# A transformer block on one core: the rotation of the queries' and keys' weights moves from VectorE and GpSimd to TensorE

## The chip, the core and the metric

The kernel runs on one core of one Trainium2 chip. The core has five engines with a queue of instructions each: TensorE (PE in the profile, with its weight loads as PEld), VectorE (DVE), ScalarE (ACT), GpSimd (POOL) and SyncE (SP), which here issues every DMA. An engine works through its own queue in order; engines wait for each other only through semaphores. Matrix products land in PSUM, everything else lives in SBUF. The metric is the device time of one execution in microseconds (us). Three runs of the kernel before gave 1052.85, 1056.75 and 1058.46 us, median 1056.75 us.

## The reference

Inputs are `x` (8, 512, 512) and the weights of one attention layer and one feed-forward layer, all in fp32. Cut to what matters:

```python
x = x + layernorm(attention(layernorm(x)))
x = x + layernorm(ffn(layernorm(x)))

# attention: 16 heads of 32; q, k, v from x @ w_attn + b_attn (512 x 1536)
q = rope(q); k = rope(k)            # the angle depends on the head and the pair, not on the token
p = softmax(causal(q @ k.T)) * 512**-0.5
out = (p @ v) @ w_proj + b_proj

def rope(a, b):                     # the two values of a pair of columns
    return a * cos - b * sin, a * sin + b * cos

# ffn: both weights made ternary (sign(round(w / mean|w|)) * mean|w|), rows normalised and
# quantised to 128 steps of their largest value, exact gelu in between
```

The rotation's angles are indexed by head, so the rotation is a fixed linear map of the columns of the projection. The kernel therefore turns the columns of `w_attn` for queries and keys once, ahead of all tokens, and never turns a query or a key.

## The kernel before, in words

The whole block runs as one program over 8 sequences of 512 tokens. `prepare_x` normalises 128 rows of `x`, splits them into an fp16 high and low half and has them transposed (by TensorE for the first sequence, L494, by transposing DMAs after it, L501). `queries_keys` makes queries and keys of a group of 4 heads with 12 fp16 products each (L553), `values` the values (L523). `maxima` makes the scores of four heads (L588, in `sc` tiles of PSUM) and takes them to SBUF with the row minima by a VectorE pass (L602). `probabilities` exponentiates (ACT, L639), rounds to fp16 (ACT, L645), takes the remainder (POOL, L647) and has both transposed by DMA. `weighted` multiplies by the values (L674), `gather` and `project` follow (L719). The feed-forward part is `ff_front`, `ff_expand` (L805, gelu L814), `ff_quantise` (L828, L839, L843, L756, L761) and `ff_contract` (L861).

The weights are prepared on the way. `make_v_weights` and `make_proj_weights` scale and split the other attention weights; `magnitude` (ACT, L410) reads the feed-forward weights a first time for their mean, and `ternarize` (POOL L446, ACT L449) makes them ternary on a second reading.

The queries' and keys' weights are made in eight pieces, one for queries (s = 0) and one for keys (s = 1) of each of four head groups g, of 512 x 128 each. `load_qk` loads one as `wraw`. `make_qk_weights(s, g)` takes the squares (ACT, L231), sums them over all 512 rows with a product by ones (PE, L240, and a one-column fp32 product for the bias, L241), turns the weights (`rotate`, L203 to L205: six passes over 128 x 256 values, by VectorE for queries and by GpSimd for keys), derives a power-of-two scale that bounds the longest column (VectorE, L249 to L256 and L170), and splits the scaled weights into two fp16 halves `wqk` (ACT L259, DVE L261). The cosines and sines lie in `cs`, spread over all partitions by one DMA (L888); `bcol` and `rcol` hold the bias and the angles with one column of weights per partition.

What sets the order of the work is the string `ORDER`: one letter is one step of one stream of work (H: queries' weights, J: keys' weights, N: `prepare_x`, T: `magnitude`, Y: `ternarize`, S: `maxima`, A: `probabilities`, X: `ff_expand`, and so on). Steps are traced in that order, and `pin` ties each instruction to the one before it on its engine, so that each queue is exactly the string's order:

```python
for k in "".join(ORDER.split()):
    step(k)
```

PSUM is shared by three `sc` tiles of two banks and two `mm` tiles of one bank. `sc` tiles are used by scores, by the product with the values and by `ff_expand`; `mm` tiles by all other products. The pool tag `x1` has five buffers and holds `wraw`, `rot`, `cs` and later rows of `x`; the tag `ph1` has two buffers for probabilities.

Of the kernel before, what the change touches and what calls it, by code (L numbers as in the profile page):

```python
# [10 lines left out]
F32 = mybir.dt.float32  # L11
# [8 lines left out]
P = 128  # L20
# [16 lines left out]
nnwwwNBtRNHnnwHHHHtttNNJJNNNNBNJJBBHBBBBwJRNHJBHwNNNJBBNTNBNHNNNNRRRHRHRBTttHHNNTwtNBRNNJTtRNHNN  # L37
TtTtJHHJJJNNTtTtHTtBQJRNNQHHHQJTtQQQJQJQTHQHQTJJTBJwQYtIttQQBQQBQJHHHTRQtTtHQSQnSHwnYYQTtYQYQAHS
YYSYtAASQYNVQYHnntrYYAAVtANVVAYYtJSSQQAAQQYQQQQAAAJJAQQVSAVVVVQVQYNtYAJAAJVAJVVVYtVAASAAArVVNSSn
AVWWJSVVVJVAAAAYVASVVVASAAAYVStSQWQQWYWWAAVAAASWAQQQQQQVVQNYYWWNNSWWWAAAAAWNNNNNVRSAAYSNSASNNWYA  # L40
QtNtVQAAAAAWARNAASAAASVVSWWYRNNNSWGSGWWWWWWWWWAAAAAAVVVVYSVVAAVVASAVWQAQAAAGGYYVVVWSWANVVSAAQSGG
QSASAQAAAAAWSWWAAQWQQQQRSWWWWWNWAAAAQWQWAYQYAAQASGAQSRQAQASAAARStQQnQQtSWWQWAAASWWWQSVGGWWWQWWWR
WWQAVAAYAGYGGSAQQAAVAAAQAVQAASQSSSQQAQAQAAQPAPYYAPPPtPQPASSAPPFAFAVPNVVVSSAPPPAFASAAAVWPVVPFFWQW
WWAQFFWVAWnANAnQQVQWWVWQQQQQNWNSYYSVPVFSWPAWAANASYNFPQNNAPAAAAAAAWNNAAAGXFAPFNNASNSAQXXFFSGXXXXX
XNXPWZrnNAnWWWAWWPVNNNWSAVASWWWWWZWVXZZVAAAAVWZPSAAAAXXVZVAFAZAZXZQSQQQSAVQSANXQQXQNPrXXPXPSPGGA
FAXGASQWPSPWZAWFQZQWWWAAAWWWGVQWWWWWVVSAQZVAZrASCAZGQZGQAAAAAZSZQQAAACSSPCZAAAACQSCZACVWVCVPFZZS
VSCAPAAAAAAQWQGWAAQSWQQWACSQACWQWCQWFASAWWWWWWSACQCZAGGVVVGSVAAQFASQQQNNAAWQQWQAQSVnQVAAVVSPVAPV
AAAAVSPVWWWCZWSPSQWWWWQWWAASFFFPQWAAAXAQXASAAXAZZAWFZAQAQQSQVXZZAPVQAPSXXWPQNNNXXAVNSNVPQWFQCXWP
WWPWAPCZFnNNFNXSFAFGFZZCFGWrAWPWCVCWCWWVWNAAZNZNNZNZFSnAACXAAZZVVSNVNWNCCVSAAAFZVPCAFVFXPXFQCSXQ
SAAACVASPAQASAAAAVVQVQXXQNZQXXAAPNSZZXPXSQXPZXCCZrPQZZSWWWPWACQACAZXCAAAAWXCWCFZAFAAPZPZQSXQFPPS  # L50
FZFFSAPZACPGACXGCGWWWWWPZXXSCZPVZGZCAAXWCZCXZACCFCFVFCWZAZZSCVAVQCQWCWQCZAQZSCAASWSACAAAGQQQSXAQ
WWWCWQNAnXQGWWWWWWWAANACCAAAAZACVAGrCPFSZWXQVSFPQFrFFGVVVSXGXGVVVVZXPFZVPXSPZAXAVZSVQFPQAAAAAAAS
PQPFWQAAAAQZQQXPXSQZZZZZCCQCQCSWWWCFFSFWWCFWPWWWWAAAWCAQQZAVWVASASCWAVVQCZSCQnAZAAXQSXXSQZZCACAA
PAAAAACSPACASXAQZPAAAQCXXZGPXXQPWPGQXCWQWQWCWZWZFNNrXXCXXZZZWWCWWWWNCAWCXFCAFPPQAAAAZZQFVFFFPNNN
NCNVnAZXXZWSXZXNZCCnCCPZCCNrNNSVZVFZXZPZZZNCPXCSXPAASNZZAPCVXCXANNASPAVSCZSACPAAZAAVZVVCZZZSVASC
ASAAAAVVQAXCCAAASCAQCSXWWQVCQFXVQFXQPWPZVrWWVQCPQNZWQPZZQAAGGZXPZAGWSANGAAQXQACPQSWWFQWXQWWQCWFC
FFZFZASSAACWWSAAZAAACQZWQFZZPCQXCQCWWWWSPXQGGZGZXQFAAAAnAAWASAAAXCCFNFCFSFSCVWWWWWVZAQAPXXWXXVCA
QWGZnZVVXSQNrXAZAGXQVQFGFSSSAQCZZVZXXAQAVVAQZSAAFQZVQVVAAXQCWQCAWCZZFAQAQFPCXSPCWCWWSPZFCPCAASAZ
PXWZZFZCAAACZZZXAAAXAWAAVXACSCVSQZPPVVSPSPAQPQWCCPWWPWWXArAZZAAQQZSPCFWFQCZAZZZQCQAACQWCZFAAQNPA
ASCWCQNWCPXGWWWXWSPQXVNAAAFCNGCZNAFWWWWWWWnZAAFFVNNWNACVXSZVVSCZNSPVAPNACSVVSFNAACFrASNPACAAAAAA  # L60
AAPPCXXCXFANXCXACZXNSZSZZNCZNPVSCVAXFFAnCVZCCAVAAAPCCAXXSZXSFQFXPFNPZCCQAPZSQWQZWXWWXFrXWXWPGGQG
# [17 lines left out]
ZZWWCWWWWWWWWGGGCXCZZZZXXCCZCXXZPCCPPPZZPPCPFrCCZCCPZZFZFFFXXZXCCPZZZFFCXCXZCFPXrZXCCZZCCZPZXZCr  # L79
PPPZPZPFFFFXZPPPPPFCPZFZZPPFCXCFXCCXZZZXZZPXFCXCXXZZFPZCXFCCFCFZXFZCXPZXCXXPCrZPZXXXPPZPZCZZZFCZ  # L80
XXFZXXZFFZZFZFCCCFCXCCCCCCZXZCZZCXCZZZZZCXCXCXXZZZZZXXCZXCXCXCCZCZZCZZCCCCXCCXCXCZCCXZXZZZCCCZZZ
CZCCCZZZZZZZCCCCCCCCCCCCCCCCCCCCCCCCCCCCC
"""


# [937 lines left out]
```

## Time and profile before

| what | value |
|---|---|
| median of three runs | 1056.75 us (1052.85 to 1058.46) |
| the profiled execution | 1060.78 us, its span 1059.0 us |
| busy: PE, DVE, ACT, POOL | 973.7, 842.0, 907.2, 795.2 us |
| first scores on PE (L588), first pass over them on DVE (L602) | 54.70 us, 55.65 us |
| first exponential on ACT (L639) | 57.31 us |
| first gelu on ACT, with its table load (L814) | 192.82 us |
| DMA packets' time, as a share of 16 engines' span | 90.7% |

Times in the profile count from the start of the span. A digit of the 40 slices is the busy share of some 26 us in tenths. In tables by stretch, each engine has its busy time in that stretch and the number of its instructions; PEclk is the granted TensorE clock as a share of full speed. A busy PE is an upper bound, since ends of matmuls are modelled. One fp32 product shows as two records, each with its own weight load; one fp16 or bf16 product shows as one.

### The profile page before, as it was taken

How to read it: one execution, taken by the hardware profiler on the slowest of the kernel's cores; microseconds unless marked ns; L12 is line 12 of the kernel's file. 1: busy time of each engine (PE TensorE's matmuls, PEld its weight loads, DVE VectorE, ACT ScalarE, POOL GpSimd, SP SyncE). 2: the span in 40 equal slices, each digit the busy share in tenths (PEclk: the TensorE clock that was granted, in tenths of full speed). 3: DMA queues.
4: the chain of work that ended last, by engine and by line, in shares of the span. 5: the costliest groups of instructions: out<-in, count | busy, mean ns of one | idle time of the engine just before them, and what ended most of it. 6: DMA issues, size and time to landing. Idle time of an engine off the chain costs nothing.

```text
span 1059.0 us, 22837 instructions
## 1 busy us (share of the span) xinstructions
PE 973.7 (92%) x8170; PEld 499.2 (47%) x8170; DVE 842.0 (80%) x2652; ACT 907.2 (86%) x1492; POOL 795.2 (75%) x648
## 2 busy tenths in 40 slices
PE   4677789998999999999999999999999999999995
PEld 2344445444545554555545455454454444444441
DVE  7988869898888788787988887797878788866651
ACT  4788989999799997999999999889899889964552
POOL 6888989888786777885888687767867768865543
PEclk9898889999999999999999999999999999999997
DMA  8779999999998998999999999899998979995452
GB/s 288 259 230 201 221 192 206 193 203 186 181 183 151 200 169 167 192 182 175 187 189 176 179 183 169 160 168 195 176 170 161 170 135 182 193 191 126 100 109 70
DMA packets 588498, 189.74 MB, mean 179 GB/s; under 512 B 564576, under 2 KB 568672, under 8 KB 588384
## 3 DMA queue, kind: packets, MB, share of 16 engines
q1 hardware_dynamic: 588384, 188.28, 90.7%
q8 instruction: 64, 1.05, 0.4%
q14 instruction: 50, 0.41, 0.1%
HBM read 38.29 MB, written 8.39 MB: 44 GB/s over the span
## 4 chain that ended last, share of the span: by engine, by line
PE 33%; ACT 15%; POOL 14%; DVE 13%; DMA 11%; issue 8%; SPq 1%; POOLq 0%; ACTq 0%; DVEq 0%
PE sc L805 10%; PE mm L861 7%; POOL ph L647 6%; PE mm L553 5%; ACT p L639 5%; DMA pT<-ph 4%; PE mm L719 4%; DVE p L602 4%; DMA qT<-q 3%; PE mm L523 3%; ACT ph L645 3%; PE sc L674 3%; PE sc L588 2%; POOL h L839 2%; DMA xT<-hT 2%
## 5 line engine op out<-in xcount | busy, mean ns | idle before, releaser
L647 POOL TENSOR_TENSOR ph<-p,ph 128x768 f16<-128x768 f32 (+1 forms) x192 | 353.0, 1841 | 81.8 <-ACT ph L645 69.2
L602 DVE CUSTOM_DVE_ANT_0 p<-sc,mask,e_scale 128x384 f32<-128x384 f32 (+3 forms) x512 | 255.4, 545 | 22.7 <-POOL ph L647 13.7
L861 PE MATMUL mm<-wout,qT 128*128 128x512 fp8e4 x1024 | 259.4, 382 | 7.9 <-DMA qT<-q 6.0
L805 PE MATMUL sc<-wfc,qT 128*128 128x512 fp8e4 x1024 | 254.7, 380 | 2.6 <-DMA qT<-q 2.4
L639 ACT ACTIVATE p<-p,nmax 128x384 f32<-128x384 f32 (+3 forms) x512 | 254.2, 551 | 2.0 <-DVE nmax L613 1.4
L553 PE MATMUL mm<-xT,wqk 128*128 128x512 f16 x768 | 207.2, 389 | 10.2 <-DVE wtop L250 3.4
L645 ACT CAST ph<-p 128x768 f16<-128x768 f32 (+1 forms) x192 | 172.6, 899 | 4.3 <-DMA pT<-ph 0.8
L805 PEld LDWEIGHTS <-qT 128*128 128x128 f16 x1024 | 97.4, 98 | 116.0 <-issue 7.9
L861 PEld LDWEIGHTS <-qT 128*128 128x128 f16 x1024 | 94.9, 98 | 118.6 <-issue 13.8
L674 PEld LDWEIGHTS <-pT 128*128 128x128 f16 x2560 | 99.0, 98 | 57.8 <-DMA pT<-ph 16.8
L674 PE MATMUL sc<-vt,pT 128*128 128x65 f16 (+1 forms) x2560 | 103.7, 187 | 12.1 <-DMA pT<-ph 9.9
L553 PEld LDWEIGHTS <-wqk 128*128 128x128 f16 x768 | 70.6, 100 | 90.4 <-issue 24.0
L523 PE MATMUL mm<-wv,xT 128*128 128x256 f16 x768 | 104.0, 276 | 4.9 <-DVE src L567 1.9
L839 POOL TENSOR_SCALAR h<-h,hnm,hqs 128x1024 f32<-128x1024 f32 x64 | 79.0, 1235 | 37.9 <-DVE hnm L835 37.8
L719 PE MATMUL mm<-wp,oT 128*128 128x512 f16 x384 | 102.0, 379 | 5.7 <-DVE row L730 1.6
L523 PEld LDWEIGHTS <-xT 128*128 128x128 f16 x768 | 73.2, 99 | 34.9 <-issue 11.2
L761 POOL TENSOR_TENSOR q<-h,q 128x1024 f16<-128x1024 f32 x32 | 69.7, 2178 | 26.5 <-ACT q L756 24.0
L588 PE MATMUL sc<-src 32*128 32x128 f16 (+3 forms) x1536 | 76.0, 303 | 13.8 <-DVE low L602 10.7
L828 DVE TENSOR_REDUCE htop<-h 128x1 f32<-128x1024 f32 x64 | 76.5, 1211 | 5.5 <-ACT h L814 5.5
L756 ACT CAST q<-h 128x1024 f16<-128x1024 f32 x64 | 66.5, 1039 | 16.6 <-POOL h L839 15.6
L814 ACT ACTIVATE h<-sc,fsc 128x1024 f32<-128x1024 f32 x64 | 71.0, 1110 | 7.4 <-PE sc L805 7.0
L843 ACT ACTIVATE junk<-h 128x1024 bf16<-128x1024 f32 x64 | 67.3, 1052 | 11.1 <-DMA qT<-q 10.2
(156 smaller groups left out, 1378.7 us busy)
## 6 DMA issues: line engine op xcount, KB each, us to landing
row<-in_x SPq DMA_DIRECT2D x32, 256.0 KB, 3.5
tw<-in_w_fcT SPq DMA_DIRECT2D x16, 512.0 KB, 5.5
tw<-in_w_outT SPq DMA_DIRECT2D x16, 512.0 KB, 4.8
x<-in_x SPq DMA_DIRECT2D x32, 256.0 KB, 3.6
out<-row SPq DMA_DIRECT2D x32, 256.0 KB, 2.8
wraw<-in_w_attn SPq DMA_DIRECT2D x8, 256.0 KB, 5.1
pT<-ph SPq DMA_TRANSPOSE x128, 5.5
qT<-q SPq DMA_TRANSPOSE x96, 4.3
```

What stands on the lines that cost most here:

```text
L523: nc.tensor.matmul(ps[:, :256], xT[:, c, hx, k, :], wv[hw][:, k, half * 256 : (half + 1) * 256], start=(n == 0), stop=(n == 3 * NE - 1),)
L553: nc.tensor.matmul(ps, w[:, hw, k, :], xT[:, :, hx, k, :], start=(n == 0), stop=(n == 3 * NE - 1),)
L588: nc.tensor.matmul(scs[j // 2][:, j % 2, at : at + (i + 1) * P], src[rows, hq, ts(i, P)], src[rows, hk, : (i + 1) * P], start=(m == 0), st ...
L602: nc.vector.tensor_tensor_reduce(p[:, j, at : at + (i + 1) * P], scs[t][:, j, at : at + (i + 1) * P], mask[:, T - (i + 1) * P :], e_scale[ ...
L639: nc.scalar.activation(pj, pj, AF.Exp, bias=nm[:, i, 2 * t + j : 2 * t + j + 1], scale=-1.0)
L645: nc.scalar.copy(hi, p)
L647: nc.gpsimd.tensor_tensor(lo, p, hi, ALU.subtract)
L674: nc.tensor.matmul(oo[:, j, i, :width], probs[u, PARTS[i]][:, half, j, STARTS[i] + c, :], vt[c][:, h, :width], start=(n == 0), stop=(n == ...
L719: nc.tensor.matmul(ps, oTs[b, k][:, ho, i, :], wp[hw][:, k, :], start=(n == 0), stop=(n == 3 * NE - 1),)
L805: nc.tensor.matmul(ps[:, o1, :], xsT[0][:, n // NE, n % NE, :], wfc[:, n % NE, ts(o, 512)], start=(n == 0), stop=(n == 2 * NE - 1),)
L839: nc.gpsimd.tensor_scalar(hh, hh, nm, s, ALU.add, ALU.mult)
L861: nc.tensor.matmul(ps, hT[0][:, half, k, :], wout[:, o2 * NF // 2 + k, :], start=(n == 0), stop=(n == 2 * NF - 1),)
```

## The change

`make_qk_weights` no longer turns the weights by elementwise passes. Four fp32 products by an identity transpose the piece into PSUM (four blocks of 128 x 128, a product with `turns[:, NG]`). ScalarE copies the transposed piece to SBUF (`wT`) and squares it with a running sum along the free axis, which gives the squared length of each column. Four more fp32 products, of `wT` with `turns[:, g]`, transpose back and turn in one: `turns[:, g]` has the cosines on its diagonal and the sines beside it, built once from `rcol` by VectorE in `qk_biases`. VectorE puts the squared lengths, with the bias added, on a diagonal (`diag`, bf16), one product by ones spreads them over all partitions, and the reduction to the largest and the scale follow as before, with one pass less. The two fp16 halves are made from the turned weights in PSUM.

`rotate`, the tile `cs` and its DMA are gone. `turns` takes a buffer of tag `ph1`. Each piece takes two `sc` tiles of PSUM, where it took one `mm` tile. `wT` takes the place of `rot` in tag `x1`. `ORDER` is another string over the same steps, shown here by its first line alone; a weight piece still takes seven steps.

```diff
-nnwwwNBtRNHnnwHHHHtttNNJJNNNNBNJJBBHBBBBwJRNHJBHwNNNJBBNTNBNHNNNNRRRHRHRBTttHHNNTwtNBRNNJTtRNHNN
...
+nnnwwwBRwNHHNwttwtNNHJHJNNJNHJNNBBBBBBBNBNHNJRwRRNBBHHntNHNHNNJHTtRJRJHJRRNTJNNBNNJtHNBNTtNHHHHN
...
@@ -180,29 +180,33 @@
     bcol = const.tile([P, 5 * NE], F32)
     rcol = const.tile([P, 4 * NE], F32)
     bqk = const.tile([P, 2 * NG], F32)
-    cs = x1p.tile([P, 2, E // 2], F32, tag="x1", name="cs")
+
+
+    turns = pp.tile([P, NG + 1, P], F32, tag="ph1", name="turns", bufs=2)
 
     def qk_biases():
 
         n = 2 * NE
-        t = tiny(n, "bt")
+        t = tiny(n + NG, "bt")
+        t, nsin = t[:, 0:n], t[:, n : n + NG]
         nc.vector.tensor_tensor(bqk, bcol[:, 0:n], rcol[:, 0:n], ALU.mult)
         nc.vector.tensor_tensor(t, bcol[:, n : 2 * n], rcol[:, n : 2 * n], ALU.mult)
         nc.vector.tensor_tensor(bqk, bqk, t, ALU.add)
-        yield
-
-    def rotate(dst, w, c, s, eng):
-
-        wv = w.rearrange("p s (f two) -> p s f two", two=2)
-        dv = dst.rearrange("p s (f two) -> p s f two", two=2)
-        a, bb = wv[:, :, :, 0], wv[:, :, :, 1]
-        shape = [P, w.shape[1], w.shape[2] // 2]
-        c, s = (t[:, None, :].to_broadcast(shape) for t in (c, s))
-        for n, (x1, x2, op) in enumerate(((c, s, ALU.subtract), (s, c, ALU.add))):
-            t = pp.tile([P, 2, *shape[1:]], F32, tag="p", name="rope", bufs=3)
-            eng.tensor_tensor(t[:, 0], a, x1, ALU.mult)
-            eng.tensor_tensor(t[:, 1], bb, x2, ALU.mult)
-            eng.tensor_tensor(dv[:, :, :, n], t[:, 0], t[:, 1], op)
+
+
+        nc.vector.tensor_copy(turns[:, NG, :], ident_h)
+        for g in range(NG):
+            nc.vector.tensor_scalar(turns[:, g, :], ident_h, rcol[:, g : g + 1], None, ALU.mult)
+            pairs = turns[:, g, :].rearrange("p (f two) -> p f two", two=2)
+            ones_at = ident_h.rearrange("p (f two) -> p f two", two=2)
+            sine = nsin[:, g : g + 1]
+            if g == 0:
+                nc.vector.tensor_scalar(nsin, rcol[:, n : n + NG], -1.0, None, ALU.mult)
+            for two in range(2):
+                nc.vector.scalar_tensor_tensor(
+                    pairs[:, :, two], ones_at[:, :, 1 - two], sine, pairs[:, :, two], ALU.mult, ALU.add
+                )
+        yield
 
     wr = w_attn.rearrange("(c p) f -> p c f", p=P)
     wqk = {
@@ -227,30 +231,32 @@
 
 
         n = s * NG + g
-        sq = tp.tile([P, NE, P], BF16, tag="q", name="sq", bufs=2)
-        nc.scalar.activation(
-            sq.rearrange("p c f -> p (c f)"), w.rearrange("p c f -> p (c f)"), AF.Square
-        )
-        yield
-        b2 = tiny(name=f"b2{s}")
+        pst = sc_tile()[:, 0, :]
+        for k in range(NE):
+            nc.tensor.matmul(pst[:, ts(k, P)], w[:, k, :], turns[:, NG, :], start=True, stop=True)
+        yield
+        wT = x1p.tile([P, E], F32, tag="x1", name="wT")
+        sq = tp.tile([P, E], BF16, tag="q", name="sq", bufs=2)
+        longest = tiny(2, f"long{s}")
+        nc.scalar.copy(wT, pst)
+        nc.scalar.activation(sq, pst, AF.Square, accum_out=longest[:, 0:1])
+        yield
+        b2 = longest[:, 1:2]
         nc.vector.tensor_tensor(b2, bqk[:, n : n + 1], bqk[:, n : n + 1], ALU.mult)
-        yield
-        ps = mm_tile()
+        nc.vector.tensor_scalar(b2, longest[:, 0:1], 2.0 * E, b2, ALU.mult, ALU.add)
+        diag = tp.tile([P, P], BF16, tag="qT4", name="diag", bufs=2)
+        nc.vector.tensor_scalar(diag, ident_h, b2, None, ALU.mult)
+        yield
+
+        ps = sc_tile()
+        rot = ps[:, 0, :]
         for k in range(NE):
-            nc.tensor.matmul(ps[:, 0:P], ones_b, sq[:, k, :], start=(k == 0), stop=(k == NE - 1))
-        nc.tensor.matmul(ps[:, P : P + 1], ones, b2, start=True, stop=True)
-        yield
-        rot = x1p.tile([P, NE, P], F32, tag="x1", name="rot")
-        at = slice(g * P // 2, (g + 1) * P // 2)
-        rotate(rot, w, cs[:, 0, at], cs[:, 1, at], nc.gpsimd if s else nc.vector)
-        rot = rot.rearrange("p c f -> p (c f)")
+            nc.tensor.matmul(rot[:, ts(k, P)], wT[:, ts(k, P)], turns[:, g, :], start=True, stop=True)
+        nc.tensor.matmul(ps[:, 1, 0:P], ones_b, diag, start=True, stop=True)
         yield
         top, sc = tiny(name=f"wtop{s}"), tiny(name=f"wsc{s}")
-        nc.vector.tensor_reduce(top, ps[:, 0:P], AX.X, ALU.max)
-        nc.vector.scalar_tensor_tensor(
-            top, top, 2.0 * E, ps[:, P : P + 1], ALU.mult, ALU.add
-        )
-        nc.vector.tensor_scalar(top, top, 2.02, 2.0**-60, ALU.mult, ALU.max)
+        nc.vector.tensor_reduce(top, ps[:, 1, 0:P], AX.X, ALU.max)
+        nc.vector.tensor_scalar(top, top, 4.04, 2.0**-60, ALU.mult, ALU.max)
         root_power(top, top)
         nc.vector.reciprocal(sc, top)
         nc.vector.tensor_scalar(sc, sc, 2.0 ** (12 - 65) / X_S, None, ALU.mult)
@@ -885,10 +891,6 @@
 
 
     def load_ropes():
-        nc.sync.dma_start(
-            out=cs.rearrange("p a f -> p (a f)"),
-            in_=rope.rearrange("a f -> (a f)").partition_broadcast(P),
-        )
         nc.sync.dma_start(out=bcol, in_=b_cols)
         nc.sync.dma_start(out=rcol, in_=rope_cols)
         yield
```

## The prediction, made before the changed kernel ran

> **What bounds the kernel now.** I read the page's slices first, then busy time by stretch, then the rows of the first 60 us, where the edited steps lie.
>
> ```profile
> PE   4677789998999999999999999999999999999995
> DVE  7988869898888788787988887797878788866651
> ACT  4788989999799997999999999889899889964552
> POOL 6888989888786777885888687767867768865543
> PEclk9898889999999999999999999999999999999997
> ```
>
> From the seventh slice (about 160 us) PE stands at nine tenths or more, with one exception, to the last but one; ACT comes near, with sevens between. Before that PE is at four to eight tenths, and its granted clock is mostly short of full. So the span is a ramp, in which PE waits for the others, and a long stretch that PE bounds. Cutting the span at the first pass over scores (55.65 us), at the first gelu's table load (192.80 us) and near the end gives (columns: stretch, its length, PE, PEld, DVE, ACT, POOL, clock, DMA share, GB/s):
>
> ```profile
> 0.00:55.65 55.65, 30.59 (x154) 15.62 (x155) 46.46 (x129) 34.89 (x60) 41.08 (x60) 0.91 0.81 270
> 55.65:192.80 137.15, 111.00 (x1128) 62.69 (x1128) 113.89 (x412) 126.06 (x218) 120.35 (x92) 0.90 1.02 208
> 192.80:1000.00 807.20, 786.02 (x6692) 401.05 (x6691) 658.74 (x2054) 724.78 (x1184) 610.15 (x476) 1.00 0.94 175
> ```
>
> I call the first two A and B. In the third PE is busy 786.02 of 807.20 us, 97.4%: what the change saves off PE there is worth nothing, and what it does in A and B moves the start of that stretch and with it the end. In B ACT is busy 92%, POOL 88%, DVE 83%, with the DMA engines' share at 1.02: four resources nearly level, ACT first. A in stretches of 8 us shows one engine ahead:
>
> ```profile
> 8.00:16.00 8.00, 4.19 (x20) 2.02 (x19) 7.55 (x24) 4.96 (x9) 7.23 (x9) 1.00 1.01 366
> 16.00:24.00 8.00, 4.22 (x12) 1.85 (x13) 7.69 (x24) 3.07 (x6) 5.34 (x4) 1.00 1.05 360
> 24.00:32.00 8.00, 5.89 (x26) 2.82 (x23) 7.06 (x18) 5.75 (x11) 7.16 (x6) 1.00 0.53 159
> 32.00:40.00 8.00, 3.82 (x19) 2.07 (x19) 7.79 (x19) 7.17 (x14) 7.03 (x9) 0.62 0.72 222
> 40.00:48.00 8.00, 5.31 (x28) 2.54 (x27) 7.67 (x19) 7.65 (x14) 6.74 (x17) 0.95 0.94 320
> ```
>
> DVE is the third number: 7.06 to 7.79 of 8 us in all five. PE is at half, ACT between, POOL at 5.3 to 7.2. So A is DVE's queue, and the chain of waits agrees: from 39 us to 48.8 us it lies on DVE alone, through rotation, scale and second halves of weights, before it passes to PE.
>
> **The change, part by part.** The rows that price it:
>
> ```profile
> 22.95 0.41 DVE L203 TENSOR_TENSOR rope<-wraw,cs 128x256 f32<-128x256 f32 x1
> 23.29 0.41 DVE L204 TENSOR_TENSOR rope<-wraw,cs 128x256 f32<-128x256 f32 x1
> 23.73 0.88 DVE L205 TENSOR_TENSOR rot<-rope 128x256 f32<-128x256 f32 x1
> 26.50 0.28 DVE L249 TENSOR_REDUCE wtop<-mm 128x1 f32<-128x128 f32 x1
> ...
> 17.32 1.06 ACT L410 ACTIVATE tw<-tw 128x1024 f32<-128x1024 f32 x1
> 18.28 0.19 ACT L410 ACTIVATION_READ_ACCUMULATOR tw<-tw 128x1 f32 x1
> ...
> 18.34 2.02 PE L339 MATMUL mm<-wpraw,bv 128*128 128x512 f32 x2
> 28.70 1.13 PE L339 MATMUL mm<-wpraw,bv 128*128 128x512 f32 x2
> ...
> 49.67 0.98 PE sc L314 x8
> ```
>
> *DVE in A.* Rotation of a query piece runs from 22.95 to 26.50 us, 3.55 us; the others take 3.64 (6.75 to 10.39), 3.43 (38.83 to 42.26) and 3.0 us (six rows at 50.83 to 53.8), together 13.6 us, all ahead of the first pass over scores. Added ahead of that pass by the new order: `turns`, five full passes of 128x128 at 0.28 us (the bias passes L335, 0.28 at their least), eight half passes at 0.22 (between 0.28 and the 0.15 of a one-column pass) and one of 0.15, 3.3 us; seven `diag` passes at 0.28, 2.0 us; seven one-column passes for the squared length against six of L250 that go, 0.15; and, moved forward, one more second half (L261, 0.75), its four small passes (0.6) and one row's statistics (0.69 and three small ones, 1.1), 2.4 us. Sum -13.6 + 3.3 + 2.0 + 0.15 + 2.4 = -5.7 us. The halves now read PSUM: L567 (PSUM in, same shape) has 0.74 beside L261's 0.75, on ACT L565 0.68 beside L259's 0.72, so nothing for that.
>
> *PE in A.* Out go 28 products by ones and 7 of one column; a piece's five take from 0.46 us (at 45.68 us) to 0.82 us (from 24.68 to 25.50), so 3.2 to 5.7 us. In come 28 transposes and 24 turns ahead of the first scores, fp32, 128x128, which no row shows. From below: four fp32 products with one weight row and one column take 0.98 us back to back (49.67 us), 0.25 each. From above: the 512-column product at 18.34 us takes 2.02 us at the slow clock, a quarter 0.51. So 13.0 to 26.5 us and 0.5 for six products by ones; net between +10.3 (13.5 - 3.2) and +21.3 (27 - 5.7). PE is busy 29.9 us ahead of the first scores at 54.70, so 24.8 us are idle, 7.4 of them before any weights have landed. With no other gap PE would come to its first scores at 7.4 + 29.9 + 10.3 = 47.6 us at the least, or 58.6 with 21.3. I take 0.35 a product, nearer the lower row, since the same 512-column product took 1.13 us at 28.70, 0.28 a quarter, and a fuller PE should hold that pace more often: 18.2 + 0.5 - 4.4 (the middle of what goes) = +14.3, 51.6 us.
>
> On the clock the rows are: four fp16 transposes in 0.61 us at 16.20 and 17.94, in 0.39 at 27.23 after 2.5 us of near steady products, in 0.63 again at 37.81 after two idle stretches over 2 us. [...] No fp32 product of this shape is in the trace to decide.
>
> *POOL.* Six passes a key piece, 24 in all at some 0.74 us, 17.8 us go; 18 of them lie in A. The last of the rows that the first queries need are split on POOL at 33.53 us, behind one rotated piece (9.27 to 14.02, 4.8 us) and two passes of L306; the new order has no rotation and one L306 ahead. They can come some 7 us sooner, but I take nothing for it, since DVE and PE then set the end of A.
>
> *ACT.* Per piece a copy from PSUM (0.65, between 0.58 for L496 and 0.72 for L259) and a square with its running sum (0.62 + the 0.19 that an accumulator read takes at 18.28) replace a square of 0.62: +0.84, eight times 6.7 us, all ahead of the first exponential in the new order. A has 20.8 idle us on ACT, 4.2 of them one wait for POOL at 18.5, so this is covered there. But four of the sixteen passes of L410 now stand behind the first exponential: 4 x 1.04 = 4.2 us more in B, less one square and one eviction (0.9) that left it: +3.3.
>
> *Queues and buffers.* SP loses one issue of 0.42 us (`cs`); a load of `x` takes its place, so the first `wraw` is no earlier. The other DMAs are the same; three of the second readings of the feed-forward weights go behind the first transposes, whose place in SP's queue is so much sooner. Pieces six and seven take four `sc` tiles between scores; a turned piece holds its tile until DVE has made its second half, and the next scores wait. That is two holds; the score waits for DVE in the trace (L588 for `low` L602) are 10.7 us over 8, 1.3 each: 0 to 2.6, I take 0 because the products of L523 and L553 stand between. `turns` holds one of two `ph1` buffers until the last turn, which stands ahead of the first cast into that tag: nothing, and if late one cast (1.04).
>
> *The sum.* A ends by DVE at 55.65 - 5.7 = 49.95, by PE's first scores at 51.6 plus 0.95 to the pass = 52.55, -3.1. PE's 29.9 us were in part at the slow pace too and would shrink, so I take a value between, -4. B: POOL's share there loses 3.0 (six rotations out, 4.4, one row's preparation out, 2.9, four L352 in, 4.3), ACT's rises 3.3 with 11.1 us idle to hide it: 0 to 3.3, I take +1. From the gelu on, order and work are the same kinds in the same numbers, so -3 reaches the end: span 1056, execution 1057.8 against 1060.78. The median of the runs stands 4.03 us below the profiled execution; 1056.75 - 3 = 1053.75, say **1053.5 us**.
>
> **The rivals.**
>
> *Faster by more.* Several DVE rows in A are far above their least: L261 once 2.63 against 0.75, L335 twice 1.0 against 0.31, L267 0.92 and 0.50 against 0.15, with POOL active at each. That is 1.9 + 1.4 + 1.1 = 4.4 us. If a lighter POOL ends these, PE's other products speed up as well, and B hides its addition, A ends 5.7 + 4.4 = 10.1 us sooner: 1046.7. Against it: the POOL passes beside four of these five rows are L306, L310 and L510, which stay; and PE would have to start its first scores at 44.6, under its least.
>
> *Slower: PE becomes the bound of A.* The place is PE's queue ahead of the first scores. At price p PE arrives there no sooner than 7.4 + 29.9 - 4.4 + 0.5 + 52p; that passes 54.70 at p = 0.41. At 0.51, with 5.7 taken out, it is 58.6, +3.9; with the middle of B's bounds, 1.7, it makes +5.6: 1062.4. For it: PE's clock in A is short of full in several rows. Against it: rows near 27 and 43 us are fast as soon as PE is busy.
>
> *No change.* DVE's time is saved but B is a level field with ACT in front; A's 3 to 4 us come back as ACT's 3.3: 1056.5.
>
> **How the numbers follow.** Chances: the forecast 0.45 (its own range 1050 to 1057), faster by more 0.22, slower 0.23, no change 0.10. About 0.5% (5.3 us) is what a measurement of this kernel can tell from no change, so faster means below 1051.5 and slower above 1062.0. Of the forecast 0.14 lies below 1051.5, and the slower case counts whole: faster 0.36, same 0.41, slower 0.23. The range runs from 1044 (the faster case and its uncertainty) to 1064 (PE's upper price), leaving out some 0.06 below and 0.10 above.
>
> **What would show it.** In the changed kernel's profile DVE's busy time up to the first pass over scores should be 40 to 42 us against 46.46, the first pass near 51.5 us; the new products 0.28 to 0.45 us each back to back; the first gelu's table load near 190 us; PE from there on as before. Wrong is the forecast if PE shows no gap before the first scores and these come after 54.7; if the first scores come by 46 us; or if the gelu is late although the scores were early, with ACT the cause. It would also fail if the rewritten order costs PE idle time after 200 us, which I could not price: it holds there only 21 us.

## The result, and the profile after

The changed kernel takes 1062.01 us, the median of six runs (1060.58 to 1065.54), beside 1056.62 us for the kernel before: a ratio of 1.0064 with a 95% interval of 1.0042 to 1.0086. It is slower, by 0.64%, where the forecast was 0.3% faster. The profiled execution took 1061.11 us, its span is 1059.0 us; the span before was 1059.0 us as well, but that execution stood 4 us above its own median, this one 1 us below. What differs by a few microseconds at the end is therefore read from the medians, and the profiles are used for where it happens.

Lines of the changed kernel lie six further down from L262 on: scores L594, their pass L608, exponential L645, product with the values L680, projection L725, expansion L811, gelu L820. The slices of its page:

```profile
PE   6875889988999999999999899999999999999997
DVE  7888679888978888887988887889779888866643
ACT  6998999988899998998899899989899889974553
POOL 5479889887868667686888577876966777864553
PEclk9996889999999999999999999999999999999999
```

In the first two slices PE is fuller (digits 6 and 8 against 4 and 6) and POOL emptier (5 and 4 against 6 and 8). Cut at the same events as before, the first pass over scores, the first gelu's table load, and near the end (stretch, length, PE, PEld, DVE, ACT, POOL, clock, DMA share, GB/s):

```profile
0.00:46.19 46.19, 33.85 (x233) 24.00 (x234) 36.02 (x136) 35.10 (x68) 22.43 (x40) 1.00 0.89 296
46.19:184.10 137.91, 109.74 (x1132) 63.34 (x1130) 109.29 (x401) 129.48 (x226) 115.38 (x88) 0.88 1.05 213
184.10:1000.00 815.90, 786.31 (x6681) 400.72 (x6679) 671.04 (x2052) 723.55 (x1180) 602.97 (x474) 0.99 0.95 172
```

Stretch A ends at 46.19 us instead of 55.65, 9.5 us sooner. B lasts 137.9 us against 137.15. The gelu's table load stands at 184.12 us, 8.7 us sooner than the 192.82 of before. So the ramp became shorter by more than was forecast, and all of it, with 5 us besides, was lost behind it. From the gelu to 1000 us PE is busy as long as before (786.31 and 786.02 us), but its idle time grew from 21.2 to 29.6 us. Two rows of 100 us show the place, before first:

```profile
300.00:400.00 100.00, 99.86 (x875) 51.64 (x873) 82.80 (x262) 96.56 (x154) 74.05 (x56) 1.00 0.99 180
400.00:500.00 100.00, 98.44 (x816) 50.38 (x815) 81.71 (x252) 91.55 (x150) 75.88 (x60) 1.00 0.96 181
```

and the changed kernel's:

```profile
300.00:400.00 100.00, 97.42 (x859) 50.26 (x857) 82.02 (x241) 90.45 (x146) 69.28 (x55) 1.00 0.92 170
400.00:500.00 100.00, 95.69 (x774) 48.13 (x773) 80.05 (x244) 93.33 (x152) 72.91 (x59) 0.98 0.92 167
```

PE, the second number, loses 2.4 and 2.8 us in these two stretches. To follow a lead through the long stretch I compare when one and the same product of the expansion starts, this kernel minus before (us; the experiments come below):

| product, at its time before | 183 | 296 | 420 | 525 | 661 | 897 | 949 | 1027 |
|---|---|---|---|---|---|---|---|---|
| changed kernel | -7.8 | -8.7 | -6.7 | -1.1 | +3.0 | +3.1 | +2.8 | +3.0 |
| run 1: its ramp, before's order behind | -7.0 | -8.7 | -8.1 | -8.4 | -7.0 | -7.8 | -3.8 | -4.2 |
| run 13: before, rotation left out | -3.1 | -5.1 | -5.4 | -5.2 | -4.6 | -5.0 | -5.3 | -5.7 |
| run 14: another join | -6.7 | -11.5 | -10.4 | -12.1 | -10.9 | -11.2 | -4.6 | -5.0 |
| run 15: one POOL pass moved | -8.2 | -13.0 | -11.8 | -13.3 | -11.8 | -13.2 | -9.5 | -9.9 |

The changed kernel's lead goes between 420 and 661 us, at no single wait. Its row scatters from product to product (+3.1 us at 426, -6.3 at 460), since the rewritten order also moves each product against the work around it: the trend counts, not one entry. The other four rows gain 2 to 5 us between 183 and 296, so that before's profiled execution, 4 us above its median, may have lost them there; the rows tell where a lead falls, and the medians how much is left at the end.

### The profile page after: what moved, and what is told of

It reads as the page before. It is cut to its first block, busy times and chain, and to the rows that moved or that the text cites. A ratio compares the mean times of both kernels' runs of the same rounds, so it can differ in the third digit from the quotient of the medians.

```text
span 1059.0 us, 22992 instructions
## 1 busy us (share of the span) xinstructions
PE 979.1 (92%) x8258; PEld 509.3 (48%) x8258; DVE 842.5 (80%) x2650; ACT 912.7 (86%) x1508; POOL 768.0 (73%) x624
## 5 line engine op out<-in xcount | busy, mean ns | idle before, releaser
L653 POOL TENSOR_TENSOR ph<-p,ph 128x768 f16<-128x768 f32 (+1 forms) x192 | 349.0, 1821 | 89.7 <-ACT ph L651 72.8
L608 DVE CUSTOM_DVE_ANT_0 p<-sc,mask,e_scale 128x384 f32<-128x384 f32 (+3 forms) x512 | 255.4, 545 | 29.1 <-PE sc L594 14.3
L811 PE MATMUL sc<-wfc,qT 128*128 128x512 fp8e4 x1024 | 255.2, 382 | 5.8 <-DMA qT<-q 3.5
L867 PE MATMUL mm<-wout,qT 128*128 128x512 fp8e4 x1024 | 255.0, 380 | 2.1 <-DMA qT<-q 1.4
L645 ACT ACTIVATE p<-p,nmax 128x384 f32<-128x384 f32 (+3 forms) x512 | 253.8, 551 | 1.3 <-DVE nmax L619 0.7
L559 PE MATMUL mm<-xT,wqk 128*128 128x512 f16 x768 | 202.0, 385 | 8.9 <-DVE vt L544 4.9
L811 PEld LDWEIGHTS <-qT 128*128 128x128 f16 x1024 | 96.9, 98 | 116.2 <-issue 9.4
L680 PEld LDWEIGHTS <-pT 128*128 128x128 f16 x2560 | 99.3, 98 | 71.4 <-DMA pT<-ph 32.5
L680 PE MATMUL sc<-vt,pT 128*128 128x65 f16 (+1 forms) x2560 | 104.7, 188 | 26.9 <-DMA pT<-ph 23.1
L845 POOL TENSOR_SCALAR h<-h,hnm,hqs 128x1024 f32<-128x1024 f32 x64 | 80.7, 1261 | 36.0 <-DVE hnm L841 33.9
L725 PE MATMUL mm<-wp,oT 128*128 128x512 f16 x384 | 101.9, 382 | 5.0 <-DVE src L573 2.0
L767 POOL TENSOR_TENSOR q<-h,q 128x1024 f16<-128x1024 f32 x32 | 68.6, 2143 | 26.3 <-ACT q L762 25.2
L594 PE MATMUL sc<-src 32*128 32x128 f16 (+3 forms) x1536 | 75.7, 307 | 6.7 <-DVE low L608 3.9
L820 ACT ACTIVATE h<-sc,fsc 128x1024 f32<-128x1024 f32 x64 | 71.1, 1110 | 5.3 <-PE sc L811 4.7
```

Of the source, the lines that this page charges most:

```text
L559: nc.tensor.matmul(ps, w[:, hw, k, :], xT[:, :, hx, k, :], start=(n == 0), stop=(n == 3 * NE - 1),)
L608: nc.vector.tensor_tensor_reduce(p[:, j, at : at + (i + 1) * P], scs[t][:, j, at : at + (i + 1) * P], mask[:, T - (i + 1) * P :], e_scale[ ...
L645: nc.scalar.activation(pj, pj, AF.Exp, bias=nm[:, i, 2 * t + j : 2 * t + j + 1], scale=-1.0)
L653: nc.gpsimd.tensor_tensor(lo, p, hi, ALU.subtract)
L680: nc.tensor.matmul(oo[:, j, i, :width], probs[u, PARTS[i]][:, half, j, STARTS[i] + c, :], vt[c][:, h, :width], start=(n == 0), stop=(n == ...
L725: nc.tensor.matmul(ps, oTs[b, k][:, ho, i, :], wp[hw][:, k, :], start=(n == 0), stop=(n == 3 * NE - 1),)
```

## The experiments

Theories at first (O, B and C in the expectations): *Order* (the rewritten `ORDER` of the long stretch costs PE time), *Bound* (the long stretch has a pace of its own that eats any lead), *Code* (the changed code slows the long stretch). Whole orders were not exchanged between the two codes, whose first parts use other buffers; instead an order is left at a step, with the rest in the other order's sequence. Ratios are against the kernel before, run on the same chip.

### Runs 1 to 4: the two halves of the order

```diff
 # run 1, changed code; run 2, before's code (X is the first expansion)
-ORDER = own
+ORDER = own[:first X] + (what is left, in the other kernel's sequence)
 # run 3, changed code
+ORDER = own[:150th X] + (what is left, in before's sequence)
 # run 4, before's code: own up to the first X, rewritten to the 150th, own again
```

> The changed kernel with its own order up to the first step of the feed-forward expansion (step 734 of 4361), and from step 744 on the order of the kernel before, letter for letter. Theory O (the lead of some 8 us at the first gelu is lost to the rewritten order of the long stretch): the lead stays, ratio to the kernel before 0.991 to 0.994 (1047 to 1050 us), PE's idle time from the gelu to 1000 us back near 21 us. Theory B (the long stretch has a bound of its own, DMA or buffers, so a lead can't be carried): ratio 0.998 to 1.004. Theory C (the changed code itself slows the long stretch, for instance because the three sc buffers come in another turn): ratio 1.004 to 1.009, as the changed kernel.

> The kernel before, its code and its order up to the first step of the feed-forward expansion, and the rewritten order from there on. Theory O: the rewritten order costs the same 10 to 15 us that the changed kernel lost between its gelu and its end: ratio 1.009 to 1.014 (1066 to 1071 us). Theory B: about 1.000 (0.998 to 1.003). Theory C: about 1.000 too, since the code is the old one; B and C are told apart by the first run.

> The changed kernel with its own order up to the 150th of 320 expansion steps (some 540 us in), then the old order. Theory O, with the loss spread evenly from 300 to 650 us: about 6 of the 10 us are lost by the join, ratio 0.997 to 1.001. Theory B: 0.998 to 1.004. Theory C: 1.004 to 1.009.

> The kernel before with the rewritten order only from the first to the 150th of 320 expansion steps (some 190 to 540 us), old order before and after. Theory O, loss spread evenly from 300 to 650 us: +6 us, ratio 1.004 to 1.008. Theories B and C: 0.998 to 1.003.

| run | median, us | ratio (95%) |
|---|---|---|
| 1: changed code and ramp, before's rest | 1055.42 | 0.9983 (0.9964 to 1.0002) |
| 2: before's code and ramp, rewritten rest | 1072.52 | 1.0137 (1.0108 to 1.0167) |
| 3: changed code, rewritten until the 150th X | 1062.93 | 1.0051 (1.0033 to 1.0069) |
| 4: before's code, rewritten between the 1st and 150th X | 1067.38 | 1.0098 (1.0070 to 1.0126) |

PE's idle time between the gelu's table load and 1000 us follows the order, 22.6 us in run 1 and 33.9 in run 2 (before 21.2, changed 29.6):

```profile
184.97:1000.00 815.03, 792.46 (x6732) 404.75 (x6731) 665.98 (x2069) 724.96 (x1183) 612.04 (x479) 1.00 0.95 174
192.80:1000.00 807.20, 773.26 (x6641) 395.47 (x6640) 668.96 (x2042) 717.96 (x1170) 598.20 (x470) 1.00 0.94 173
```

Of the ratios expected under *Order* only run 2's came; run 1 fell into *Bound*'s range, run 3 into *Code*'s, and run 4 above *Order*'s. What decides is that runs 2 and 4 differ from the kernel before in the order alone, and so does run 1 from the changed kernel. That the order costs time is settled. With before's code the rewritten rest costs 1.4%, by the ratio 14.5 us; behind the changed ramp it costs 0.8% (1.0064 against 0.9983), and most of that by the 150th expansion (1.0051), in the stretch where the table shows the lead going. Run 1 also shows a second loss: with before's order behind it the ramp's 8 us are there until 897 us in the trace, but the median is only 0 to 4 us better.

### Runs 6 and 7: is the rewritten order bad, or any other order?

```diff
 # before's code; each step behind the first X between its two places, a (rewritten) and b (before's)
-place = b
+place = 0.75 * b + 0.25 * a      # run 6; run 7: 0.25 * b + 0.75 * a
```

> Before's code and before's order up to the first expansion. Behind it each step stands a quarter of the way from its place in before's order to its place in the rewritten order (as the second experiment has it, which cost 14.5 us in full). The code, the counts and the ramp are those of before. Theory Moves (the cost sits in what the rewritten order moves, in proportion to how far): +2 to +5 us against before. Theory Any (before's order fits its own timing closely, and any shift of the interleaving among engines loses what it had): most of the cost at once, +7 to +15. Theory Other (the cost is made by the largest moves alone): within 2 us of before.

> As the experiment before it, but three quarters of the way to the rewritten order. Theory Moves: +8 to +13 us against before. Theory Any: +7 to +18, about the same as at a quarter. If it comes out within 4 us of before, the loss belongs to a few moves that the last quarter completes.

Run 6 took 1095.11 us, 1.0370 (1.0349 to 1.0390), run 7 1097.72 us, 1.0391 (1.0372 to 1.0410). Both are worse than either end. At a quarter a step stands on average 1.9 places from before's, and that costs 39 us, far above what any theory had said; *Moves* falls, *Any* holds in kind. So a mixture of the two orders is far worse than either, and the rewritten one is merely the poorer of the two by about 1%. Not every small shift costs: run 15 below moves one POOL pass with its transposes and loses nothing. That the steps and their counts are the same says nothing about the time at this level.

### Runs 5, 10 and 11: what made the ramp shorter

All three are run 1 with one thing added to its preparation of weights.

```diff
 # run 5: each of the fp32 products twice, into the same place
+            for _ in range(2):
                 nc.tensor.matmul(pst[:, ts(k, P)], w[:, k, :], turns[:, NG, :], start=True, stop=True)
 # run 10 (run 11: if s, nc.gpsimd): passes that nothing waits for
+        if not s:
+            six_passes(nc.vector, g)
```

> The kernel of the first experiment (changed code, its order up to the first expansion, before's order behind it) with each of the 52 fp32 products of 128x128 issued twice into the same place, so that the second overwrites the first with the same numbers. What is tested is the slower rival of the prediction: that PE's queue of fp32 products becomes the bound of the ramp once a product costs more than 0.41 us; two products of 0.26 us are 0.52. Theory Bound (the rival's own sum, with no other gap than the first wait): 52 x 0.26 = 13.5 us more PE work ahead of the first scores, which then come at least 6 us later than in the first experiment's profile (44 to 46 us). Theory Slack (PE still waits for DVE, POOL and the loads, and the second product fills these waits): first scores 0 to 3 us later, and less than half of the 13.5 us shows. At the end, by Bound, the run is 3 to 8 us slower than the first experiment (1055.42 us); by Slack 0 to 3.

> The kernel of the first experiment, with six passes over 128x256 fp32 with a step of two on DVE put back into the preparation of each query piece, ahead of its scale, where the rotation was. They read and write memory that is not used before 104 us, so nothing waits for their data; they cost DVE time alone, about 0.41 us each, 10 us for the 24. Theory DVE (as the prediction had it: the ramp is DVE's queue, and what is taken off it ends the ramp sooner): first scores 5 to 10 us later than the 45.4 us of the first experiment. Theory PE (behind the change PE's queue sets the first scores, DVE is busy 35 of the first 46 us and has room): first scores 0 to 4 us later.

> As the experiment before it, on POOL and for the key pieces: 24 passes over 128x256 fp32 at about 0.74 us, 17.8 us, which the prediction took off POOL at a gain of nothing. Theory Nothing (as predicted): first scores within 1 us of 45.4. Theory POOL (the rows and biases that POOL makes come that much later, and passes of DVE and POOL that run beside each other take longer on both): first scores 3 to 10 us later, the half passes over rows, 1.16 us each in the first experiment, back near 1.4, and DVE passes above their least again.

The added passes, by the groups of run 10 and then of run 11 in their first 80 us (busy, mean ns of one):

```profile
L217 DVE TENSOR_TENSOR wout<-wout 128x256 f32<-128x256 f32 x24 | 15.4, 640 | 0.7
```

```profile
L217 POOL TENSOR_TENSOR wout<-wout 128x256 f32<-128x256 f32 x24 | 15.0, 623 | 1.6
```

| run | first scores, us | gelu's table load | median | ratio (95%) |
|---|---|---|---|---|
| 1 | 45.45 | 184.97 | 1055.42 | 0.9983 (0.9964 to 1.0002) |
| 5: products twice | 51.64 | 192.21 | 1060.77 | 1.0050 (1.0035 to 1.0066) |
| 10: 15.4 us on DVE | 58.31 | 202.47 | 1073.60 | 1.0162 (1.0124 to 1.0200) |
| 11: 15.0 us on POOL | 50.49 | 193.09 | 1060.54 | 1.0043 (1.0020 to 1.0066) |

DVE's time is worth most, 12.9 us of ramp for 15.4 us of passes, more than *DVE* had said because a pass took 0.64 us and not 0.41. POOL's is worth 5.0 us for 15.0: *Nothing*, which was the prediction's step, falls, though one mark of *POOL* is missing: its half passes over rows stayed at 1.16 us. The doubled products delay the first scores by 6.2 us, just inside what *Bound* (here PE's queue as the bound of the ramp) had said, although that is less than half of the 13.5 us added. The rest went into waits: PE's pauses over a quarter microsecond in the first 60 us, behind its first wait, shrink from 4.9 to 1.5 us.

### Runs 9, 12 and 14: the change with as much of before's order as it takes

```diff
 # changed code
-ORDER = own
+ORDER = own[:n] + (what is left, in before's sequence)   # run 9: n = 169, run 12: 297, run 14: 330
```

> Changed code with the rewritten order only up to the first scores (its first 169 steps); behind that before's order for what is left, letter for letter the same from step 282 on, where the first experiment goes over at 744. So this is the change with before's order wherever that can be kept. Theory Code (the fp32 products and the lighter DVE and POOL shorten the ramp whatever the order behind): first scores 44 to 46 us, gelu table load 5 to 9 us before the 192.8 of before, and 2 to 6 us faster than before at the end. Theory Fit (each order holds its time only with the ramp that it stands behind): the first scores are early all the same, but the stretch from there to the gelu or the long one gives the lead back, and the time is between 1056 and 1075 us.

> As the run before the last two, with the join later: the rewritten order up to the last step of the keys' weights (297 steps), before's order for what is left, the same letter for letter from step 369. Theory Code: 2 to 6 us faster than before, and within 2 us of the run that joins at the first scores. Theory Fit: the two joins differ by over 3 us although the code and nine tenths of the order are the same, and neither need be faster than before.

> As the runs that join the two orders at the first scores (169 steps, ratio 0.9997) and at the last key weights (297 steps, 0.9983): changed code, the rewritten order up to the first product with the values (330 steps), before's order for what is left, the same letter for letter from step 389. It asks whether the point of the join matters, and is a candidate for a version faster than both. Theory Code (only the code's shorter ramp counts, not the join): within 2 us of 1054 to 1056 us. Theory Join (the place where two orders meet decides what is left of the lead): off that by more than 3 us, to either side.

| run | gelu's table load, us | median | ratio (95%) |
|---|---|---|---|
| 9: first scores | 182.75 | 1056.12 | 0.9997 (0.9981 to 1.0012) |
| 12: last key weights | 184.68 | 1053.90 | 0.9983 (0.9963 to 1.0003) |
| 14: first product with the values | 184.93 | 1052.81 | 0.9952 (0.9929 to 0.9975) |

The ramp is short in all of them, by 8 to 10 us, and the time is not slower than before: the changed code by itself does not cost time. But it keeps 0 to 5 us of the lead, by where the orders meet; the intervals of runs 9 and 14 do not touch, so *Join* has a part beside *Code*. By the times expected it is less clear: run 9 has *Fit*'s, run 12 falls between the two theories, and run 14's median of 1052.81 us still lies in *Code*'s range; only its ratio sets it apart. Run 14 is faster than both kernels.

### Run 13: does a lead carry at all?

```diff
 # before's code and before's order, rotate()
-            eng.tensor_tensor(t[:, 0], a, x1, ALU.mult)
-            eng.tensor_tensor(t[:, 1], bb, x2, ALU.mult)
-            eng.tensor_tensor(dv[:, :, :, n], t[:, 0], t[:, 1], op)
+        eng.tensor_copy(dst, w)
```

> Before's code and before's whole order, with the six passes of each rotation (DVE for queries, POOL for keys) replaced by one copy of the same rows, so that queries and keys are not turned: that part of the computation is left out. It makes the ramp of before's own kernel shorter without any other step changing place, and asks what a sooner start is worth to the long stretch under the order that was written for before. DVE loses about 3 us and POOL 3.5 to 4 us a piece; gelu table load 4 to 9 us before 192.8. Theory Carry (the stretch behind the ramp takes its time from PE and keeps any lead; what the first, ninth and twelfth runs lost there, 5 to 8 us, is due to the changed code or to the join of two orders): the whole lead shows at the end, 4 to 9 us faster than before. Theory Fit (an order holds the long stretch only with the entry that it was written for; engines that come in sooner, and not all by as much, meet each other's buffers at other moments): less than half of the lead shows, 0 to 4 us faster.

The lead at the gelu is 3.1 us (189.7), less than the 4 to 9 that was expected; the median is 1052.59 us, 0.9967 (0.9948 to 0.9986), 3.5 us better, and the table's row keeps its lead to the end. *Carry* holds in kind, though 3.5 us is less than its 4 to 9, and *Bound* (a pace of the long stretch of its own) falls: under its own code and order the long stretch passes a sooner start on, and in full as far as an interval of 1.5 to 5.5 us can tell.

### Runs 8, 15 and 16: where the second half of the lead goes

In runs 1, 5, 8, 9, 11, 12 and 14, all of the changed code under before's order, 3 to 7 us of lead go between 897 and 949 us. (Runs 5, 8 and 9 lose 4 to 6 us between 525 and 661 us besides, where the longest wait of PE, 1.9 to 3.0 us, is for a transposed tile of probabilities; no run was aimed at that.) Run 8 moved the loads of residual rows.

```diff
 # run 8, on run 1: each r (load of a residual row) behind step 1200 six steps sooner
 # run 15, on run 14
-... A733 Z332 Z333 Z334 Q383 Q384 S279 P217 W417 P218 W418 A734 A735 A736 ...
+... A733 Z332 Q383 Q384 S279 P217 W417 P218 W418 A734 A735 Z333 Z334 A736 ...
 # run 16, on run 14
-... P215 F180 S278 F181 X241 Q382 X242 P216 W414 ...
+... P215 F180 P216 S278 F181 X241 Q382 X242 W414 ...
```

> The kernel of the first experiment with each load of the residual rows (second reading of x) behind step 1200 put six steps sooner in the order, nothing else. In the first experiment's profile the lead of the shorter ramp is 8 us until 890 us and 4 behind it; at 891 us DVE waits 0.82 us for such a load, its pass then takes 2.30 us beside a POOL pass, and PE stands 2.32 us for DVE at the projection. Theory Load (that late load is what costs the second half of the lead): the stop at 894 us goes, the lead is 6 to 8 us at the end, and the time falls 2 to 4 us below 1055.42, to 1051.5 to 1053.5. Theory Moved (a stop taken away here comes back at the next place where the engines meet): the stop at 894 us goes or shrinks, and the time stays within 2 us of 1055.42.

> The kernel of the fourteenth run with one POOL pass (the second half of a quantised row, 2.13 us, with the transposes that read it) put behind the next POOL pass of the probabilities, nothing else. In that kernel's profile DVE's pass for the residual row, 0.75 us in 24 of its 32 instances, took 2.45 us at 888 us, 0.67 us idle ahead of it, beside that POOL pass, and PE then stood 2.32 us at the projection; the lead against before fell from 11 to 5 us between 890 and 945 us. Theory Overlap (the DVE pass is held by the POOL pass that began just ahead of it): the DVE pass takes 0.75 to 1.2 us, the stop at 892 us falls below 1 us, the profile keeps 1 to 3 us more of its lead, and the median is 1 to 3 us under that of the fourteenth run. Theory Elsewhere: the DVE pass is short but PE's stop stays or comes back within 50 us, and the median is the same within 2 us.

> The kernel of the fourteenth run with the step of that residual row (a one-column POOL pass and the DVE pass behind it) put ahead of four other steps, so that DVE makes it before the passes over scores that stood ahead of it. Theory Overlap: the DVE pass no longer stands beside the 2.13 us POOL pass; PE's stop of 2.32 us falls below 1 us; median 1 to 3 us under that of the fourteenth run. Theory Elsewhere: the pass waits for POOL at its new place (its input is ready only at 886.4 us, beside another POOL pass that lasts to 888.0), the scores behind it come 1 to 2 us later, and the median is the same or up to 3 us above.

Run 8 took 1055.79 us, 1.0005 (0.9986 to 1.0023), with a stop of 2.22 us at the same product. It was no test of the load: the load was still issued right behind a transpose of probabilities of 4.15 us, at 890.21 us, and DVE waited 1.45 us for it. The place in the timeline of run 14 (start, length, engine, instruction, idle time ahead of it):

```profile
886.40 1.64 POOL L653 TENSOR_TENSOR ph<-p,ph 128x768 f16<-128x768 f32 x1
...
888.00 2.13 POOL L767 TENSOR_TENSOR q<-h,q 128x1024 f16<-128x1024 f32 x1
...
888.23 2.45 DVE L745 SCALAR_TENSOR_TENSOR x<-row,pr,x 128x512 f32<-128x512 f32 x1 [0.67 <-DMA x<-in_x]
...
892.46 0.81 PE L725 MATMUL mm<-wp,oT 128*128 128x512 f16 x3 [2.32 <-DVE src L573]
```

The load of the residual row lands at 888.2 us, and POOL's L767 has begun 0.2 us earlier. The DVE pass then ends at 890.7, 0.55 us behind POOL's, with a length of 2.45 us; the median of its 32 instances is 0.75. DVE's queue, behind it the half of queries (L573), and so PE come late. In run 15 POOL's L767 stands one POOL pass further back:

```profile
884.41 1.64 POOL L653 TENSOR_TENSOR ph<-p,ph 128x768 f16<-128x768 f32 x1
886.28 0.75 DVE L745 SCALAR_TENSOR_TENSOR x<-row,pr,x 128x512 f32<-128x512 f32 x1 [0.71 <-DMA x<-in_x]
887.31 1.64 POOL L653 TENSOR_TENSOR ph<-p,ph 128x768 f16<-128x768 f32 x1 [1.26 <-ACT ph L651]
...
888.82 0.81 PE L725 MATMUL mm<-wp,oT 128*128 128x512 f16 x3 [0.67 <-DVE src L573]
...
888.90 2.15 POOL L767 TENSOR_TENSOR q<-h,q 128x1024 f16<-128x1024 f32 x1
```

The same wait for the load, 0.71 us, but the pass takes 0.75 us and PE's stop is 0.67. The lead stays at 13 us until 927 us and ends at 9.9; what is left of the loss is mostly another stop, 2.1 us at 930 us, where PE waits for a transposed tile of probabilities; its cause stays open. The median is 1048.53 us, 0.9937 (0.9914 to 0.9960). *Overlap* holds. In time alone runs 14 and 15 are not apart, their intervals overlap; the trace shows the stop gone. Run 16 put the DVE pass ahead, where it waits at the head of its queue:

```profile
886.83 2.12 POOL L767 TENSOR_TENSOR q<-h,q 128x1024 f16<-128x1024 f32 x1
887.30 2.19 DVE L745 SCALAR_TENSOR_TENSOR x<-row,pr,x 128x512 f32<-128x512 f32 x1 [2.45 <-DMA x<-in_x]
```

DVE waits 2.45 us, the pass takes 2.19 us beside the same POOL pass, PE stops for 4.20 us at 887, and the time is 1055.46 us, 0.9999 (0.9983 to 1.0015): *Elsewhere*, as described, with the load in the place of the POOL input that I had named.

Run 15 is the best kernel of the study: 0.63% faster than before, where the change as given is 0.64% slower.

## Why the prediction was wrong, point by point

**The step that failed** is "From the gelu on, order and work are the same kinds in the same numbers, so -3 reaches the end". The rewritten order moves nearly every step of the long stretch, and that costs 14.5 us behind before's ramp (run 2) and some 8.6 behind the new one (the ratios of the changed kernel and run 1, 0.0081 of 1056). In its place the runs showed PE's idle time from the gelu to 1000 us grown from the 21 us that the prediction counted on to 29.6, and back at 22.6 with before's order (run 1). The prediction named this only in its last sentence, as something it could not price, and gave it no place in the range or the chances; the median fell inside the range by luck of the other errors. Why the rewritten order is poorer is not settled; its largest group of PE's waits between 200 and 1000 us, for transposed probabilities, is 9.3 us against 6.0.

**A, -4 against -9.5.** The directions of DVE and PE were right; their sizes were not, and POOL's part was put at nothing:

*DVE, -5.7.* Busy time up to the first pass fell from 46.46 to 36.02 us, below the 40 to 42 forecast. Of the rest the second halves are a clear part. The prediction costed them at nothing because both rows have 0.75 at their least. By line (lowest, median and highest ns), before and after:

```profile
L261 DVE SCALAR_TENSOR_TENSOR wqk<-rot,wsc,wqk x8: 733/872/2626, 14.9 to 84.6; 128x512 f16<-128x512 f32 x8
```

```profile
L267 DVE SCALAR_TENSOR_TENSOR wqk<-sc,wsc,wqk x8: 740/742/745, 18.5 to 75.3; 128x512 f16<-128x512 f32 x8
```

Not the least moved but the spread: with one input in PSUM instead of SBUF every one of the eight takes 0.74 us. The five in A before had a mean of 1.19, so this is 2.2 us. The "faster by more" rival had that mechanism and blamed a lighter POOL alone; with 15 us of passes back on POOL (run 11) their mean is still 0.744, and in the changed kernel two of the eight began 0.2 and 1.0 us behind a POOL pass of 2.5 and 2.1 us and took 0.74 all the same. Its other rows came as well: the four bias passes (L335, now L341) took 1.13 us instead of 2.55, and the small L267 (now L273) 0.47 for three instead of 1.42 for two. Against that, the eight half passes of `turns` and the seven `diag` passes took 3.1 and 3.3 us, where the sum had 1.8 and 2.0.

*PE, 0.35 a product.* A group of four shows as eight records, beside the first sixteen of the span and the first scores and pass:

```profile
6.80 3.78 PE L236 MATMUL sc<-turns,wraw 128*128 128x128 f32 x16 [6.80 <-DVE turns L197]
...
17.11 1.11 PE L236 MATMUL sc<-turns,wraw 128*128 128x128 f32 x8
...
37.39 1.05 PE L254 MATMUL sc<-turns,wT 128*128 128x128 f32 x8
...
44.29 0.67 PE L594 MATMUL sc<-src 32*128 32x128 f16 x24
...
46.19 0.34 DVE L608 CUSTOM_DVE_ANT_0 p<-sc,mask,e_scale 128x128 f32<-128x128 f32 x1
```

So 0.26 to 0.28 us each in the two later rows (0.26 to 0.30 over all groups of four up to the first scores) and 0.47 for the very first eight: the lower row was the right one. First scores came at 44.29, under the 47.6 that the prediction called the least, because PE's other products, the same in number ahead of the first scores, became shorter too. Before, and the changed kernel:

```profile
L553 PE MATMUL mm<-xT,wqk 128*128 128x512 f16 x36 | 11.8, 477 | 6.1 <-DVE wtop L250 3.4 <-ACT xT L496 2.7
```

```profile
L559 PE MATMUL mm<-xT,wqk 128*128 128x512 f16 x36 | 8.4, 379 | 0.6 <-ACT xT L502 0.4 <-DVE xT L502 0.2
```

With the lines L339, L494 and L289 (now L345, L500 and L295) this makes 17.7 us of PE's time out of 25.2. L553's 3.4 us of these 7.5 go with the granted clock. Before, it is 0.50 from 34.0 to 40.7 and from 51.0 to 54.4 us, where 14 of the 36 products begin and take 0.57 to 0.63 us each; the other 22 take 0.38 to 0.43. The changed kernel shows 1.00 from 11.4 us to the end of A, and a mean of 0.38. The other three lines were slow mostly ahead of 27 us, where the profile shows 1.00, also at the 2.02 us row of 18.34 us that the prediction put down to a slow clock: what made them slow there is not shown. The denser queue goes along with the shorter products, as the prediction had expected of its 0.35, but no run separates it. A bound that adds busy times of the trace before, where these four lines took 7.5 us more, is not a bound. The doubled products of run 5 put the size on it: the rival's formula gives 7.4 + 29.9 - 4.4 + 0.5 + 52 x 0.52 = 60.4 us, measured 51.64.

*POOL, nothing.* Worth 5.0 us of ramp (run 11).

**B, +1.** It was +0.8; ACT's busy time in B rose by 3.4 us, where the prediction had 3.3.

**The rivals.** *Faster by more* is what the ramp did, and run 15, 9.4 us sooner at the gelu, keeps some 6.7 us of it by its ratio. *Slower* by PE did not happen: the price stayed below its threshold, and the loss came from elsewhere.

## What to carry to other kernels

Where an order is written out step by step, price the rewritten order as a part of the change: here, with PE at 97%, orders for the same steps differed by 9 to 41 us. Run the new code with the old order wherever it fits, and the old code with the new order, before judging the idea. A sooner start was kept where code and order stayed as they were (run 13), and lost in part at places where engines met otherwise; follow one product's lead through the trace, and look at the place where it falls. To relieve VectorE, count not only passes but which of them read two operands from SBUF while GpSimd works: here a second half took 1.19 us on the mean in A with both in SBUF, 0.74 with one in PSUM.

## What the runs showed of the hardware that was not expected

DVE's residual pass has its inputs in SBUF, and so have the POOL passes L653 and L767 (L638 and L752 in run 13). Its median is 0.75 us; it took 2.45 us (run 14) and 2.19 us (run 16) where a POOL pass of 2.13 and 2.12 us had begun 0.2 and 0.5 us sooner. In run 13 it began 0.5 us ahead of that POOL pass, which then took 2.57 us, beside a median of 2.13 before (L761 there); its own 1.11 us end 0.55 us behind the POOL pass before (L638), which had begun 1.1 us sooner and ended at 894.13:

```profile
892.49 1.64 POOL L638 TENSOR_TENSOR ph<-p,ph 128x768 f16<-128x768 f32 x1
...
893.57 1.11 DVE L730 SCALAR_TENSOR_TENSOR x<-row,pr,x 128x512 f32<-128x512 f32 x1
...
894.10 2.57 POOL L752 TENSOR_TENSOR q<-h,q 128x1024 f16<-128x1024 f32 x1
```

In all three cases the DVE pass ends 0.54 to 0.55 us behind the POOL pass that was running when it began. The same holds for the eight of the 32 residual passes before (L739) that took over 0.8 us, 0.84 to 1.75, and for the 2.63 us of L261, which ends 0.55 us behind a POOL pass of L310. Not every POOL pass did this: three of the 32 began while a one-column pass of 0.54 to 0.55 us (L150) ran on POOL, and took 0.75 each. The time lies inside the passes, apart from the wait by semaphore ahead of them (0.67 us for the load in run 14): in these traces the two engines held each other by more than semaphores.

L261 and L267 fit this: with both inputs in SBUF the eight second halves took 0.73 to 2.63 us, with one in PSUM 0.74 each, also 0.2 and 1.0 us behind the start of a POOL pass. The prediction would have needed this for the second halves; it priced them by their least.
